# Five PSUM banks in turn behind the last sampling, and coarser steps beside the samplings

## The chip, the cores and the metric

One core of one Trainium2 chip. The metric is the device time of one launch in microseconds (us), the median of the runs shown; one further execution was recorded by the hardware profiler.

## The reference, cut to what matters

Four residual layers on x of shape (4, 256, 64, 64), each behind a group norm:

```
x = x + L0(gn(x))   # 1x1 conv; 3x3 depthwise -> offsets and masks; bilinear sampling at
                    # 4 groups x 9 points of every pixel; out-projection; squeeze-excite; MLP
x = x + L1(gn(x))   # qkv 1x1 conv; 5x5 depthwise of all 768 channels; linear attention; projection
x = x + L2(gn(x))   # 3x3 conv, 256 -> 256, binarised weights
x = x + L3(gn(x))   # attention of 4096 queries over 1024 pooled keys, softmax
```

All of it is float32. The sampling of L0 reads 4096 x 9 x 4 table rows of 256 values per image, at addresses that the offsets decide.

## The kernel before, in words

The channels lie on the 128 partitions in two halves (`KT = 2`), pixels on the free axis, in blocks of 512 (`NB = 8`). The four images are worked on as a pipeline. `sample(n, ...)` is the sampling of image n: 293 rounds of 14 pixels x 9 points. A round is four indirect DMAs that GpSimd issues (L520, tile `g`, 7 buffers), 16 small matmuls that weigh and sum them (L527, tile `acc`), and, once every two rounds (`UR = 2`), a ScalarE copy `at` (L532), two TensorE transposes into `dp` (L537) and ScalarE copies into `dT` (L552). Rounds are grouped in 19 blocks of up to 224 pixels. At the end of a block the output projection (L560, tile `po`), an addition on VectorE (L564) and a scaling with a running sum on ScalarE (L569) follow; in the kernel before these three lie in successive rounds, for each of the two halves of the channels.

The rest of the work is written as Python generators that `yield` a cost at points where other work may be put in. `beside(steps, number, *works)` runs one round of the sampling, then advances each work until its costs add up to its share of the rounds gone by: beside image n's sampling stand the MLP of image n-1 (`feed`, first fifth of the rounds), L1 of image n-1 (`linear`, the other four fifths) and L2 and L3 of image n-2 (`second`, the same four fifths). `LINEAR`, `SECOND` and `OFFSETS` are the sums of the costs. Beside image 0's sampling stands the preparation (convolution, depthwise, offsets) of images 1 to 3.

During the four samplings the order on TensorE, VectorE, ScalarE and GpSimd is the order written (`manual_schedule`); SyncE's DMAs are free. Behind the last sampling (image 3's) no such order is set: the framework's scheduler orders the instructions of each engine by their place in the program and by when it believes them ready. This last part holds MLP and L1 of image 3 with L2 and L3 of image 2 beside them, and then L2 and L3 of image 3 alone.

L1's 5x5 depthwise is 25 VectorE instructions of 128x1024 for each of 24 tiles of an image (L176, tile `agg`, in PSUM). At each of its steps L1 also takes one piece from a list `later`: transposes and sums (`vk`), or the output's parts `dens`, `head`, `proj` (L788 to L812). L2's convolution is 18 matmuls for each of 16 PSUM tiles (L864), whose result VectorE adds to the residual (L855). L3's attention is, for each of 32 groups of 128 queries: scores `s` (L943), VectorE maxima `mx` (L944, L945), ScalarE exponentials `pe` (L950), transposes `pt` (L958) with ScalarE copies `pT` (L959), and the sum over keys (L963).

PSUM has eight banks. The pool `mm` has three, shared by every common tile that `ps()` gives out; `acc` and `dp` of the sampling have one each, each used as two halves in turn; `agg` has two and `vk` one. Behind the last sampling `acc` and `dp` are idle.

Of the kernel before, what the change touches and what calls it, by code (L numbers as in the profile page):

```python
# [9 lines left out]
F32 = mybir.dt.float32  # L10
# [7 lines left out]
P = 128  # L18
# [17 lines left out]

CONVOLVE, OFFSETS = NB * 17 + 18, NCH * 60
FEED = NB * 40 + 8  # L40
LINEAR = 1130
SECOND = 631
EPS_BN = 1e-5
EPS_GN = 1e-5
EPS_ATT = 1e-5
# [24 lines left out]
class Net:  # L70
    def __init__(self, ctx, tc, a, out):
        self.tc, self.nc, self.a, self.out = tc, tc.nc, a, out
        e = ctx.enter_context
        self.cp = e(tc.tile_pool(name="const", bufs=1, side="left"))
        self.gp = e(tc.tile_pool(name="gather", bufs=2, side="left"))
        self.sp2 = e(tc.tile_pool(name="samp", bufs=2, side="left"))
        self.ps1 = e(tc.tile_pool(name="ps1", bufs=1, space=PSUM))
        self.mm = e(tc.tile_pool(name="mm", bufs=3, space=PSUM))
        self.dp = e(tc.tile_pool(name="scratch", bufs=1, space=DRAM))


    def ps(self, name="ps"):
        return self.mm.tile([P, 512], F32, name=name, tag="mm")

    def rsqrt(self, pool, v, eps, cols, name):

# [82 lines left out]
    def depthwise(self, acc, src, w, k, rows, cols, r0, bias=None, step=lambda cost: cost):  # L169

        nc = self.nc
        for t in range(k * k):
            s = src[:, r0 + t // k:r0 + t // k + rows, t % k:t % k + cols]
            wt = w[:, t:t + 1]
            if t:
                nc.vector.scalar_tensor_tensor(acc, s, wt, acc, ALU.mult, ALU.add)  # L176
            elif bias is not None:
                nc.vector.tensor_scalar(acc, s, wt, bias, ALU.mult, ALU.add)
            else:
                nc.vector.tensor_scalar(acc, s, wt, None, ALU.mult)  # L180
            if t % 3 == 2 or t == k * k - 1:
                yield step(3.9)


    def setup(self):
# [208 lines left out]
    def offsets(self, n, c, y, mw, bp, used):  # L394

        nc = self.nc
        t = bp.tile([P, KT, 1024], F32, name="t", bufs=1)
        for k in range(KT):
            acc = self.ps1.tile([P, 16, W], F32, name="agg", tag="agg")
            yield from self.depthwise(acc, y[:, k], self.w3[:, k], 3, 16, W, 0, bias=self.sh[:, 2 + k:3 + k])  # L400
            yield 2
            nc.scalar.activation(t[:, k], acc.rearrange("p r w -> p (r w)"), AF.Identity, scale=SLOPE)
            yield 2
            nc.vector.tensor_tensor(t[:, k], acc.rearrange("p r w -> p (r w)"), t[:, k], ALU.max)  # L404
            yield 3
        used.append(c)
        off = bp.tile([P, CT, 2 * Q], F32, name="off")
        ml = bp.tile([P, CT, Q], F32, name="ml")
        for h in range(2):
            ps = self.ps().rearrange("p (j o) -> p j o", o=P)  # L410
            for j in range(4):
                at = (4 * h + j) * P
                for k in range(KT):
                    nc.tensor.matmul(ps[:, j, 0:3 * Q], t[:, k, at:at + P], mw[:, k], start=k == 0, stop=k == KT - 1)  # L414
            ob = self.row("offmask_b").unsqueeze(1).to_broadcast([P, 4, 3 * Q])
            nc.vector.tensor_tensor(off[:, 4 * h:4 * h + 4], ps[:, :, 0:2 * Q], ob[:, :, 0:2 * Q], ALU.add)
            nc.vector.tensor_tensor(ml[:, 4 * h:4 * h + 4], ps[:, :, 2 * Q:3 * Q], ob[:, :, 2 * Q:3 * Q], ALU.add)
            yield 3
        yield from self.coordinates(bp, n, c, off, ml)
# [56 lines left out]
    def sample(self, n, ssum):  # L476
# [3 lines left out]

        nc, sp = self.nc, self.sp2
        table = self.tab[n].rearrange("g y x s c -> (g y x) (s c)")
        blocks, images, at, dp, dT, po, later = {}, {}, {}, {}, {}, {}, {}

        def halves(name):

# [52 lines left out]
        def spread(unit, b, u):  # L539

            if b not in dT:
                p0, np_ = BLOCKS[b]
                dT[b] = sp.tile([P, G, BP], F32, name="dT", bufs=1)
                images[b] = sp.tile([P, KT, BP], F32, name="yb")
                nc.sync.dma_start(images[b][:, :, 0:np_], self.y_d[n][:, :, p0:p0 + np_])
            full = sum(1 for _, m in unit if m == RP)
            for v0, v1, m in ((0, full, RP), (full, len(unit), unit[-1][1])):
                for s in range(2):
                    if v0 < v1:
                        hs = slice(64 * s, 64 * s + 64)  # L550
                        q0 = RP * (unit[0][0] + v0)
                        nc.scalar.copy(  # L552
                            dT[b][hs, :, q0:q0 + m * (v1 - v0)].rearrange("p g (v o) -> p g v o", o=m),
                            dp[u][hs, v0:v1, :, s, 0:m].rearrange("p v g o -> p g v o"))

        def project(b, m):
            np_ = BLOCKS[b][1]
            po[m] = self.ps("po")
            for k in range(G):
                nc.tensor.matmul(po[m][:, 0:np_], self.ow[:, k, m * P:(m + 1) * P], dT[b][:, k, 0:np_], start=k == 0, stop=k == G - 1)  # L560

        def add(b, m):
            ym = images[b][:, m, 0:BLOCKS[b][1]]
            nc.vector.tensor_tensor(ym, po[m][:, 0:BLOCKS[b][1]], ym, ALU.add)  # L564

        def finish(b, m):
            p0, np_ = BLOCKS[b]
            ym = images[b][:, m, 0:np_]
            nc.scalar.activation(ym, ym, AF.Identity, bias=self.sh[:, 4 + m:5 + m],  # L569
                                 scale=self.inv[:, 4 + m:5 + m], accum_out=ssum[:, m, b:b + 1])  # L570
            if m == KT - 1:
                nc.sync.dma_start(self.x2_d[n][:, :, p0:p0 + np_], images[b][:, :, 0:np_])

        load(0)
        order = [(b, r) for b, (_, np_) in enumerate(BLOCKS) for r in range(-(-np_ // RP))]
# [1 line left out]
        for i, (b, r) in enumerate(order):  # L577
# [14 lines left out]
            if r % UR == UR - 1 or ends:  # L592
                unit = rounds[r - r % UR:r + 1]
                todo = [partial(moved, acc, len(unit), i), partial(turned, len(unit), i), partial(spread, unit, b, i)]
                todo = list(enumerate(todo, i + 1))
                if ends:
                    todo += [(i + 4 + m + j, partial(f, b, m)) for m in range(KT) for j, f in enumerate((project, add, finish))]
                for j, f in todo:
# [235 lines left out]
    def layer2(self, n, st, st3):  # L834
        nc, tc = self.nc, self.tc
        with tc.tile_pool(name=f"ca{n}", bufs=1, side="left") as sp, \
# [4 lines left out]
            before = []  # L841
            for b in range(NB):

                lo, hi = max(8 * b - 1, 0), min(8 * b + 9, H)
# [9 lines left out]
                def leave(m, ps, xv, b):  # L854
                    nc.vector.tensor_tensor(xv[:, m], xv[:, m], ps, ALU.add)  # L855
                    if m == KT - 1:
                        self.stats(st3, xv, b)
                        nc.sync.dma_start(self.x5_d[n][:, :, b * 512:(b + 1) * 512], xv)

                for m in range(KT):  # L860
                    ps = self.ps()
                    for i in range(KT * 9):
                        k, t = i // 9, i % 9
                        nc.tensor.matmul(ps, w[:, k, t, m * P:(m + 1) * P], xp[:, k, t // 3:t // 3 + 8, t % 3:t % 3 + W],  # L864
                                         start=i == 0, stop=i == KT * 9 - 1)
                        if i % 3 == 2:
                            if before:
                                before.pop()()
                            yield 2.7
                    before.append(partial(leave, m, ps, xv, b))  # L870
            before.pop()()


    def layer3(self, n, st):
        nc, tc, a = self.nc, self.tc, self.a
        M = HW // 4
        with tc.tile_pool(name=f"na{n}", bufs=1, side="left") as sp, \
# [59 lines left out]
            for b in range(NB):  # L937
                m2 = bp.tile([P, 512], F32, name="m2")
                for j in range(4):
# [3 lines left out]
                        nc.tensor.matmul(s[i], tv[:, 4 * b + j], ph[:, i * 512:(i + 1) * 512], start=True, stop=True)  # L943
                        nc.vector.tensor_reduce(mx[:, i:i + 1], s[i], AX.X, ALU.max)  # L944
                    nc.vector.tensor_scalar(mx[:, 2:3], mx[:, 0:1], mx[:, 1:2], -1.0, ALU.max, ALU.mult)  # L945
                    yield 1.5
                    pe = bp.tile([P, M], F32, name="pe")
                    den = bp.tile([P, 3], F32, name="den3")
                    for i in range(2):
                        nc.scalar.activation(pe[:, i * 512:(i + 1) * 512], s[i], AF.Exp, bias=mx[:, 2:3], accum_out=den[:, i:i + 1])  # L950
# [23 lines left out]
    def run(self):  # L974
# [159 lines left out]
```

## Time and profile before

| | |
|---|---|
| median of 3 runs | 8708.86 us (8706.62 to 8726.91) |
| profiled execution: its own time | 8708.86 us |
| profiled execution: span, first to last instruction | 8706.8 us |
| gathers of image 0, 1, 2, 3: first to last | 247.6-1870.4, 1870.8-3399.2, 3399.5-5066.3, 5066.6-6749.1 us |
| busy over the span: TensorE, VectorE, ScalarE, GpSimd | 73%, 60%, 23%, 53% |
| mean granted TensorE clock | 0.836 |

The shares are means over stages that are bound by different things: GpSimd works only until 6749 us, so the kernel has two parts, the samplings and the 1958 us behind them, and each is to be read by itself.

### The profile page before, as it was taken

The page shows a single profiled execution, that of the slowest core. Times are in us where ns is not written, and L with a number is a line of the kernel's source. Part 1 is how long each engine was busy: PE and PEld are TensorE (multiplying, and loading weights), DVE is VectorE, ACT ScalarE, POOL GpSimd, SP SyncE. Part 2 cuts the span into 40 slices and gives each one's busy share as a digit, 9 for nine tenths or more (in the row PEclk, how much of TensorE's full clock was granted, in tenths as well). Part 3 has the DMA queues.
Part 4 walks back from the last instruction along what each step waited for, and adds up shares of the span by engine and source line. Part 5 has one row for each costly group of instructions (what it writes and reads, how often), then busy time and mean ns, then how long its engine had stood idle before and what let it go on. Part 6 is the DMA issues. An engine that isn't in the chain of part 4 may idle for free. (4 is left out here: it accounts for less than half of the span.)

```text
span 8706.8 us, 92673 instructions
## 1 busy us (share of the span) xinstructions
PE 6339.9 (73%) x35276; PEld 3432.2 (39%) x35276; DVE 5243.8 (60%) x6279; ACT 2014.2 (23%) x4710; POOL 4578.5 (53%) x4694
## 2 busy tenths in 40 slices
PE   4645545569676677998767779897677898667887
PEld 2333322334333333444444434444444444334345
DVE  7445353342678775258777732778777268989213
ACT  1111111112222122222232322222322222222113
POOL 0667767677777776777776557777755000000000
PEclk7666766779767688999988989998888999889999
DMA  5556555554444454455544354555433211101210
GB/s 157 165 153 170 152 154 157 142 156 144 136 120 127 119 145 136 144 155 140 155 132 119 111 150 137 159 150 152 126 111 107 90 53 46 44 32 41 57 60 29
DMA packets 817660, 1052.57 MB, mean 121 GB/s; under 512 B 464064, under 2 KB 524608, under 8 KB 815424
## 3 DMA queue, kind: packets, MB, share of 16 engines
q0 software_dynamic: 225024, 614.77, 24.4%
q1 hardware_dynamic: 592192, 431.89, 17.3%
q8 instruction: 279, 4.57, 0.2%
q14 instruction: 165, 1.35, 0.0%
HBM read 878.36 MB, written 167.90 MB: 120 GB/s over the span
## 5 line engine op out<-in xcount | busy, mean ns | idle before, releaser
L520 POOL DMA_INDIRECT g<-tab,sl x4688 | 4577.8, 976 | 2169.9 <-issue 1295.2
L176 DVE SCALAR_TENSOR_TENSOR agg<-pad,vec,agg 128x1024 f32<-128x1024 f32 x2560 | 3295.3, 1287 | 69.1
L527 PE MATMUL acc<-g,wm 128*32 128x128 f32 x18752 | 1221.6, 319 | 1186.6 <-ACT at L532 762.0
L527 PEld LDWEIGHTS acc<-g,wm 128*32 128x32 f32 x18752 | 609.5, 121 | 1845.7 <-ACT at L532 984.7
L864 PE MATMUL ps<-xp,w 128*128 128x512 f32 x2304 | 1062.3, 608 | 80.7 <-DVE xp L848 52.8
L864 PEld LDWEIGHTS ps<-xp,w 128*128 128x128 f32 x2304 | 425.7, 192 | 565.5 <-issue 530.8
L552 ACT COPY dT<-dp 64x112 f32<-64x112 f32 x1176 | 287.1, 244 | 1328.9 <-PE dp L537 935.3
L511 DVE TENSOR_TENSOR wm<-con,sl 128x1024 f32<-128x1024 f32 (+1 forms) x296 | 357.5, 1208 | 223.5 <-PE acc L527 221.3
L645 PE MATMUL ps<-x2f,f 128*128 128x512 f32 x1024 | 477.3, 615 | 4.0 <-ACT f L636 4.0
L167 DVE SCALAR_TENSOR_TENSOR hm<-ps,vec,lk 128x512 f32<-128x512 f32 x256 | 192.2, 751 | 436.2 <-ACT lk L166 436.1
L652 PE MATMUL ps<-hm,f 128*128 128x512 f32 x1024 | 453.6, 597 | 0.0
L166 ACT ACTIVATE lk<-ps,low 128x512 f32<-128x512 f32 x320 | 219.8, 687 | 980.9 <-PE ps L645 558.2
L700 PE MATMUL ps<-xr,qw 128*128 128x512 f32 x768 | 418.1, 675 | 12.3 <-DMA xq<-x 3.2
L958 PE MATMUL pt<-ident,pe 128*128 128x128 f32 x1024 | 187.6, 330 | 228.2 <-ACT pe L950 226.1
L950 ACT ACTIVATE pe<-s,mx 128x512 f32<-128x512 f32 x256 | 173.8, 684 | 712.9 <-DVE mx L945 712.8
L414 PE MATMUL ps<-mw,t 128*128 128x108 f32 x512 | 96.5, 364 | 306.9 <-DVE t L404 306.9
L963 PE MATMUL ps<-gt,pT 128*128 128x128 f32 x2048 | 309.6, 314 | 5.6 <-ACT pT L959 3.1
L963 PEld LDWEIGHTS ps<-gt,pT 128*128 128x128 f32 x2048 | 287.9, 224 | 49.4 <-ACT pT L959 20.0
L653 DVE TENSOR_TENSOR xyf<-xyf,ps 128x512 f32<-128x512 f32 x64 | 44.0, 688 | 430.9 <-PE ps L652 430.9
L560 PE MATMUL po<-dT,ow 128*128 128x224 f32 (+1 forms) x1216 | 284.6, 383 | 24.6 <-DVE yb L564 13.2
L532 ACT COPY at<-acc 128x256 f32<-128x256 f32 (+1 forms) x588 | 218.5, 372 | 313.9 <-PE acc L527 304.8
L645 PEld LDWEIGHTS ps<-x2f,f 128*128 128x128 f32 x1024 | 192.1, 194 | 233.2 <-issue 224.5
(224 smaller groups left out, 7096.4 us busy)
## 6 DMA issues: line engine op xcount, KB each, us to landing
x<-x SPq DMA_DIRECT2D x160, 512.0 KB
g<-tab,sl POOLq DMA_INDIRECT x4688
xr<-x SPq DMA_DIRECT2D x96, 512.0 KB
x<-in_x SPq DMA_DIRECT2D x64, 512.0 KB
tab<-xo SPq DMA_DIRECT2D x512, 64.0 KB
y<-yc SPq DMA_DIRECT2D x32, 512.0 KB
x2f<-x SPq DMA_DIRECT2D x32, 512.0 KB
xyf<-x SPq DMA_DIRECT2D x32, 512.0 KB
```

The costliest lines, as they stand in the source:

```text
L166: nc.scalar.activation(t, ps, AF.Identity, bias=low, scale=SLOPE)
L176: nc.vector.scalar_tensor_tensor(acc, s, wt, acc, ALU.mult, ALU.add)
L511: nc.vector.tensor_tensor(wm[:, 0:nu], self.con("own").unsqueeze(1).unsqueeze(1).to_broadcast(sh), sl[:, r:r + nu, G:].unsqueeze(3).to_bro ...
L520: nc.gpsimd.indirect_dma_start(out=g[:, i, :], out_offset=None, in_=table, in_offset=bass.IndirectOffsetOnAxis(ap=sl.bitcast(I32)[:, r, i: ...
L527: nc.tensor.matmul(acc[32 * i:32 * i + 32, :], wm[:, r4, 4 * i + 2 * x:4 * i + 2 * x + 2, :], g[:, i, x * P:(x + 1) * P], start=x == 0, st ...
L552: nc.scalar.copy(dT[b][hs, :, q0:q0 + m * (v1 - v0)].rearrange("p g (v o) -> p g v o", o=m), dp[u][hs, v0:v1, :, s, 0:m].rearrange("p v g ...
L560: nc.tensor.matmul(po[m][:, 0:np_], self.ow[:, k, m * P:(m + 1) * P], dT[b][:, k, 0:np_], start=k == 0, stop=k == G - 1)
L645: nc.tensor.matmul(ps, f1[:, k, m * P:(m + 1) * P], x2[:, k], start=k == 0, stop=k == KT - 1)
L652: nc.tensor.matmul(ps, f2[:, k, m * P:(m + 1) * P], hm[:, k], start=k == 0, stop=k == 4 * KT - 1)
L700: nc.tensor.matmul(ps, qw[:, k, t * P:(t + 1) * P], x[:, k], start=k == 0, stop=k == KT - 1)
L864: nc.tensor.matmul(ps, w[:, k, t, m * P:(m + 1) * P], xp[:, k, t // 3:t // 3 + 8, t % 3:t % 3 + W], start=i == 0, stop=i == KT * 9 - 1)
L963: nc.tensor.matmul(ps[:, 0:P], pT[:, m], gt[:, m], start=m == 0, stop=m == 7)
```

## The change: what it does

It is two edits in opposite places. First, behind the last sampling `ps()` hands out banks in the turn `mm, acc, mm, dp, mm`, five in all, where it was the three of `mm` throughout. Second, the fine steps of the kernel before are replaced by coarser ones:

- a depthwise yields after 5 taps where it yielded after 3 (in L1 and in the preparation), and two yields around the preparation's activation go;
- L2's convolution is two steps of 9 matmuls for each tile where it was six of 3, and the addition L855 follows its own tile's last matmul at once, where it lay behind the third matmul of the next tile;
- L3's exponentials follow the maxima in the same step, where a yield of 1.5 lay between;
- the block's projection, addition and scaling come in one round, for both halves of the channels one after the other, into the halves of the bank `dp` and no longer into `mm`; the residual tile `yb` has one buffer where it had two;
- the sums `OFFSETS`, `LINEAR` and `SECOND` are set to the new costs.

```diff
-CONVOLVE, OFFSETS = NB * 17 + 18, NCH * 60
+CONVOLVE, OFFSETS = NB * 17 + 18, NCH * 55
-LINEAR = 1130
-SECOND = 631
+LINEAR = 1068
+SECOND = 612
...
+        self.banks = cycle(["mm"])
     def ps(self, name="ps"):
-        return self.mm.tile([P, 512], F32, name=name, tag="mm")
+        tag = next(self.banks)
+        return (self.mm if tag == "mm" else self.ps1).tile([P, 512], F32, name=name, tag=tag)
...
-            if t % 3 == 2 or t == k * k - 1:
-                yield step(3.9)
+            if t % 5 == 4 or t == k * k - 1:
+                yield step(6.5)
...
-            yield 2
             nc.scalar.activation(t[:, k], acc..., AF.Identity, scale=SLOPE)
-            yield 2
...
-                images[b] = sp.tile([P, KT, BP], F32, name="yb")
+                images[b] = sp.tile([P, KT, BP], F32, name="yb", bufs=1)
...
-        def project(b, m):
-            np_ = BLOCKS[b][1]
-            po[m] = self.ps("po")
+        def project(b):
+            for m in range(KT):
+                projected(b, m)
+        def projected(b, m):
+            (p0, np_), yb = BLOCKS[b], images[b]
+            po = next(dps)
             for k in range(G):
-                nc.tensor.matmul(po[m][:, 0:np_], ...)
-        def add(b, m):
...
-        def finish(b, m):
+                nc.tensor.matmul(po[:, 0:np_], ...)
+            nc.vector.tensor_tensor(ym, po[:, 0:np_], ym, ALU.add)
             nc.scalar.activation(ym, ym, AF.Identity, ...)
...
-                if ends:
-                    todo += [(i + 4 + m + j, partial(f, b, m)) for m in range(KT) for j, f in enumerate((project, add, finish))]
+                for j, f in enumerate(todo + [partial(project, b)] * ends, i + 1):
...
-                        if i % 3 == 2:
-                            if before:
-                                before.pop()()
-                            yield 2.7
-                    before.append(partial(leave, m, ps, xv, b))
+                        if i == 8:
+                            yield 8
+                    nc.vector.tensor_tensor(xv[:, m], xv[:, m], ps, ALU.add)
+                    yield 8
...
-                    yield 1.5
...
-                    yield 2
+                    yield 3
...
+        self.banks = cycle(["mm", "acc", "mm", "dp", "mm"])
         beside(range(64), 64, *behind(N - 1), (second(N - 2), SECOND, 0.2, 1))
```

More of the change, by code (lines that the diff above doesn't have):

```diff
@@ L482, in sample @@
         table = self.tab[n].rearrange("g y x s c -> (g y x) (s c)")
-        blocks, images, at, dp, dT, po, later = {}, {}, {}, {}, {}, {}, {}
+        blocks, images, at, dp, dT, later = {}, {}, {}, {}, {}, {}
         def halves(name):
@@ L554, in spread @@
                             dp[u][hs, v0:v1, :, s, 0:m].rearrange("p v g o -> p g v o"))
-        def project(b, m):
-            np_ = BLOCKS[b][1]
-            po[m] = self.ps("po")
-            for k in range(G):
-                nc.tensor.matmul(po[m][:, 0:np_], self.ow[:, k, m * P:(m + 1) * P], dT[b][:, k, 0:np_], start=k == 0, stop=k == G - 1)
-        def add(b, m):
-            ym = images[b][:, m, 0:BLOCKS[b][1]]
-            nc.vector.tensor_tensor(ym, po[m][:, 0:BLOCKS[b][1]], ym, ALU.add)
-        def finish(b, m):
-            p0, np_ = BLOCKS[b]
-            ym = images[b][:, m, 0:np_]
+        def project(b):
[4 more added lines that the diff above has]
+            po = next(dps)
+            for k in range(G):
+                nc.tensor.matmul(po[:, 0:np_], self.ow[:, k, m * P:(m + 1) * P], dT[b][:, k, 0:np_], start=k == 0, stop=k == G - 1)
+            ym = yb[:, m, 0:np_]
+            nc.vector.tensor_tensor(ym, po[:, 0:np_], ym, ALU.add)
             nc.scalar.activation(ym, ym, AF.Identity, bias=self.sh[:, 4 + m:5 + m],
@@ L571, in finish @@
             if m == KT - 1:
-                nc.sync.dma_start(self.x2_d[n][:, :, p0:p0 + np_], images[b][:, :, 0:np_])
+                nc.sync.dma_start(self.x2_d[n][:, :, p0:p0 + np_], yb[:, :, 0:np_])
         load(0)
@@ L594, in sample @@
                 todo = [partial(moved, acc, len(unit), i), partial(turned, len(unit), i), partial(spread, unit, b, i)]
-                todo = list(enumerate(todo, i + 1))
-                if ends:
-                    todo += [(i + 4 + m + j, partial(f, b, m)) for m in range(KT) for j, f in enumerate((project, add, finish))]
-                for j, f in todo:
+                for j, f in enumerate(todo + [partial(project, b)] * ends, i + 1):
                     later.setdefault(j, []).append(f)
@@ L840, in layer2 @@
             sc, bi = yield from self.groupnorm(sp, st, "g2")
-            before = []
             for b in range(NB):
@@ L853, in layer2 @@
                 xv = self.block(bp, self.x4_d[n], b, "x4")
[L854 to L858, printed above, removed]
                 for m in range(KT):
@@ L865, in layer2 @@
                                          start=i == 0, stop=i == KT * 9 - 1)
-                        if i % 3 == 2:
-                            if before:
-                                before.pop()()
-                            yield 2.7
-                    before.append(partial(leave, m, ps, xv, b))
-            before.pop()()
+                        if i == 8:
+                            yield 8
+                    nc.vector.tensor_tensor(xv[:, m], xv[:, m], ps, ALU.add)
+                    yield 8
+                self.stats(st3, xv, b)
+                nc.sync.dma_start(self.x5_d[n][:, :, b * 512:(b + 1) * 512], xv)
     def layer3(self, n, st):
```

## The prediction, made before the changed kernel ran

> **What bounds the kernel now.** I first read the list of costliest groups, then split the span into stages and asked for the busy time of each engine in them, since the page's shares mix stages.
>
> ```profile
> 247.60:1870.40 1622.80, 881.71 (x6278) 518.38 (x6278) 718.76 (x962) 249.10 (x686) 1151.40 (x1172) 0.67 0.56 155
> 1870.40:3399.20 1528.80, 1103.95 (x6733) 544.32 (x6733) 996.56 (x969) 343.00 (x855) 1145.37 (x1173) 0.77 0.46 134
> 3399.20:5066.30 1667.10, 1341.03 (x8404) 726.65 (x8397) 1099.17 (x1274) 456.68 (x1102) 1141.77 (x1172) 0.91 0.47 137
> 5066.30:6749.00 1682.70, 1351.96 (x8479) 733.57 (x8478) 1104.47 (x1288) 463.52 (x1116) 1139.19 (x1172) 0.91 0.48 138
> 6749.00:7044.00 295.00, 268.62 (x768) 125.42 (x766) 88.64 (x152) 66.73 (x116) 0.05 (x1) 0.96 0.25 77
> 7044.00:7438.00 394.00, 344.09 (x1005) 171.60 (x1006) 338.05 (x346) 83.32 (x149) 0.00 (x0) 0.92 0.17 49
> 7438.00:8138.00 700.00, 475.49 (x1662) 280.36 (x1661) 582.99 (x710) 195.63 (x379) 0.00 (x0) 0.84 0.12 38
> ...
> 8404.00:8706.80 302.80, 220.41 (x1040) 154.69 (x1040) 98.22 (x256) 108.03 (x232) 0.00 (x0) 0.94 0.14 46
> ```
>
> The columns are stretch, length, then busy time (and count) of PE, PEld, DVE, ACT, POOL, then clock and DMA. Rows 1 to 4 are the samplings of images 0 to 3 (S0 to S3). POOL is busy some 1142 us in each and spends about 0.3 us of issue between two gathers (332.8 us in S1), so a sampling cannot be shorter than about 1470 us, 5.02 us a round. S1 is 55 us above this floor, S0 150, S2 and S3 about 200. Next I asked what POOL, PE and ACT waited for in S3 (us in total, times, longest):
>
> ```profile
> POOL g L520 <- PE acc L527: 212.8, 88, 10.9
> PE acc L527 <- ACT at L532: 167.6, 76, 14.7
> ACT pe L950 <- DVE mx L945: 187.3, 22, 18.1
> ```
>
> This is a chain. POOL waits for a free `g`, which PE frees; PE waits for ACT's copy of `acc`; ACT stands in front of an exponential whose maximum VectorE has not reached. By time, POOL's waits lie in the first rounds and, some 115 us of them, in the last 59 rounds, where L1's output and L3's attention meet. Two pairs of stretches from there, and L2's convolution beside S3:
>
> ```profile
> 6334.00:6429.00 95.00, 80.70 (x408) 40.07 (x409) 64.33 (x79) 30.56 (x70) 46.83 (x49) 0.90 0.37 108
> 6429.00:6465.00 36.00, 19.85 (x172) 14.91 (x170) 34.76 (x40) 8.61 (x24) 24.14 (x25) 0.86 0.38 114
> 6465.00:6559.00 94.00, 78.70 (x405) 39.45 (x406) 62.26 (x79) 28.54 (x65) 46.07 (x49) 0.91 0.36 104
> 6559.00:6593.00 34.00, 20.66 (x171) 14.55 (x170) 33.26 (x37) 10.29 (x28) 22.75 (x25) 0.80 0.44 132
> 5534.00:5948.00 414.00, 376.91 (x2355) 192.26 (x2358) 328.73 (x320) 108.01 (x266) 314.43 (x324) 0.97 0.52 147
> ```
>
> 49 gathers are 12 rounds: where the pieces of L1's output are taken, a round lasts 7.8 us and PE is 85% busy; where they have run out, it lasts 5.8 us and DVE is 97% busy. Beside the convolution POOL does not wait (324 gathers in 414 us is 5.1 us a round), although PE is 91% and DVE 79% busy: the seven buffers `g` hide short stalls.
>
> Behind the samplings the MLP is PE's (rows 5), the mixed stretch 7044 to 8138 is DVE's (921 of 1094 us), the convolution alone PE's, and the last attention nobody's: PE 73%, DVE 32%. Its timeline, one group of queries:
>
> ```profile
> 8562.53 1.98 PE L943 MATMUL s<-ph,th 128*128 128x512 f32 x4
> 8565.58 0.69 ACT L950 ACTIVATE pe<-s,mx 128x512 f32<-128x512 f32 x1 [4.38 <-DVE mx L945]
> 8566.42 1.33 PE L958 MATMUL pt<-ident,pe 128*128 128x128 f32 x8 [1.90 <-ACT pe L950]
> 8567.80 2.05 PE L963 MATMUL ps<-gt,pT 128*128 128x128 f32 x16
> ```
>
> Scores, exponential, transposes, sum, then the next group's scores: 7.17 us to the next `pt`, of which PE idles 1.9.
>
> **What the Trainium skill says.** "PSUM — Partial Sum Buffer", section on bank collisions: two engines may not use one bank in the same quadrant at a time, at other addresses of it either, so such accesses must be kept apart by waits. The trace agrees: PE, about to write one half of `acc`, waits for ACT's copy of the other (the 167.6 us above). The same page, section "Engine vs sequencer instructions": the queues of ScalarE, VectorE and GpSimd are strict first-in first-out; the 187.3 us of ACT and the copies behind them are that. "Perfetto Trace Analysis", "Optimizing Scalar/DVE Operations": where these engines aren't saturated but cause bubbles on others, breaking work up may let it complete sooner. Here that holds for DVE (65% over S3), and the change goes the other way. The same page, "Identifying Performance Opportunities": a repeating gap can mean too little PSUM for the next tile. The 1.9 us above repeats 32 times; no run shows yet that banks are its cause.
>
> **The change part by part**, against the profiled execution's own 8708.9 us (span 8706.8; the median is the same execution). No engine's arithmetic changes; all costs are waits.
>
> *Exponentials with their maxima.* The second work is given 631/(0.8 x 293) = 2.69 units a round, so the yield of 1.5 put the exponential behind a round's boundary in 1.5/2.69 = 56% of the cases: 18 of 32 groups of an image lose that. ACT then waits while VectorE does the chunk written before, 5 x 1.29 = 6.5 us, and the maxima, 2 x 0.68 + 0.21 = 1.6 us. Half of them stand before a copy `at`, which PE needs. In the last 59 rounds (10 of the 18) I take 5 us each for 5 of them, elsewhere `g` hides most: 30 us an image in S2 and S3. Bounds: 0 (VectorE ahead) and 18 x 8.1 = 146.
>
> *Projection at once and in `dp`.* Its 8 matmul records a half, the addition (0.38 us) and the scaling are the same. New is that PE's second half, and the next transposes `dp`, wait for VectorE's additions in the same bank: at least about 0.6 us twice a block, plus VectorE's lag, 0 to 6.5 us, say 3, where it is busy. Behind PE stand the matmuls of `acc`; behind ACT, whose scaling waits likewise, the copies `at`. About 4.2 us of PE for each of 14 blocks beside L1 in S2 and S3; the last four count in full (17), the rest is in PE's idle time and `g`: 20 an image, 8 in S1, 7 in S0. SP's load of `yb` now waits for the store of the block before, but is wanted 11 rounds later: nothing, unless other loads queue behind it; that would add a few us. Bounds: 0 and 19 x 8 = 152 a sampling.
>
> *Five taps a step.* VectorE is up to 2 x 1.29 = 2.6 us later with everything behind a chunk: weights `wm`, maxima, additions. About ten places in the last rounds: 25 us an image. Against it, `later` gives one piece a step, and steps come less often: 4.56/6.5 = 0.70 a round, before 4.83/3.9 = 1.24. The 13 pieces of an output take 15.5 rounds of 18, before 10. PE's need, (80.70 + 19.85)/18.5 = 5.4 us a round, would be even, as would DVE's, (64.33 + 34.76)/18.5 = 5.4. If nothing stalled, the last rounds would fall from 7.0 to 5.4: 59 x 1.6 = 95 us an image gained. In-order waits keep most of it; I take a third, -30. In the preparation the steps already come in one burst, since it waits for its tiles and catches up; nothing there.
>
> *Convolution in two steps.* 288 matmuls take 279 us an image, so a step is 8.7 us of PE, before 2.9. VectorE's addition now stands in its queue until its own tile is done: up to 8 us, 16 times, with chunks of the depthwise queued behind. The stretch has 414 - 329 = 85 us of VectorE idle per image, which covers most: 20 an image; bounds 0 and 80. Two of the three `mm` banks are less held, worth a few us.
>
> *Banks behind the samplings.* In the last attention, five tiles a group and five banks let the next scores start once the exponentials have read theirs. If both go ahead of the sum, the group is PE-bound, 1.98 + 1.33 + 2.05 = 5.4 us: 32 x 1.8 = 57 us gained. If the scheduler puts only the first ahead, 5 to 10; if none, 0. I take 30. In the mixed stretch DVE idles 173 us, about 46 of them in the drain after the last depthwise tile and some 40 in two holes; I take 20, bounds -20 and 60 (the fixed turn can also make a tile wait for one held bank, and the coarser steps move the order). MLP and convolution alone: nothing, PE is full.
>
> Sum: S2 and S3 each 30 + 20 + 25 - 30 + 20 = 65, S0 and S1 15 together: +145; behind them -50. 8708.9 + 95 = 8804 us.
>
> **The rivals.** *Evenness wins* (faster): the spread of L1's pieces pays for all new waits. Then the samplings are level (S2, S3 at -10 each, S0 and S1 +10) and the part behind gives 57 + 20: 8709 - 10 - 77 = 8622 us. For it: the 7.8 and 5.8 us rounds side by side. Against: every piece still passes a chain PE, ACT, DVE in order, and DVE at 5.4 us a round has no slack. It decides when the samplings lose less than the attention gains. *The banks change no order* (the change doesn't do what it says): the exponential is still waited for by the transposes, the gain behind is 0: 8709 + 145 = 8854 us. *Lockstep* (much slower): waits for projection, exponentials and convolution sums add up as PE and DVE both run above 90%; S2 and S3 lose 130 each: 8709 + 275 - 40 = 8944 us. *A draw*: loss and gain cancel.
>
> **How the numbers follow.** A measurement of this kernel can tell about 0.3%, 26 us, from no change. Chances: 0.48 for the forecast (own range 8740 to 8870), 0.15 for no new order, 0.08 for lockstep, 0.20 for evenness, 0.09 for a draw. Slower 0.71, same 0.09, faster 0.20. The range reaches into the faster case and most of the way to lockstep: 8640 to 8920.
>
> **What would show it.** POOL's wait for PE `acc` should rise from 192.6 (S2) and 212.8 (S3) to about 260 to 280 each, ACT's wait for `mx` above 187.3, DVE's wait for PE at L855 above 23.4, and PE or ACT should wait for DVE at the projection's addition. The 7.8 and 5.8 us rounds should move together. Behind the samplings, PE's wait for `pe` at L958 in the last attention, now
>
> ```profile
> PE pt L958 <- ACT pe L950: 63.0, 32, 4.0
> ```
>
> should fall, with `s` of the next group before L963. I am wrong if the samplings don't lengthen, or if that wait stays and the last stretch keeps its 303 us.

## The result, and the profile after

The changed kernel takes 9070.43 us (median of 4 runs, 9065.32 to 9074.08) against 8707.74 us for the kernel before (4 runs): ratio 1.0412, 95% interval 1.0394 to 1.0430. It is slower, by 363 us, where 95 were forecast. The profiled execution, one of the four, has a span of 9067.9 us, 361 more than before's 8706.8 (also one of its four).

In the views PE is TensorE, DVE is VectorE, ACT is ScalarE and POOL is GpSimd. The four samplings again, S0 to S3, with the columns of the prediction's first table:

```profile
247.70:1877.10 1629.40, 878.66 (x6260) 513.84 (x6260) 722.29 (x967) 252.13 (x689) 1152.29 (x1172) 0.68 0.55 155
1877.40:3407.40 1530.00, 1056.57 (x6734) 529.30 (x6734) 997.85 (x964) 342.46 (x852) 1151.31 (x1172) 0.77 0.46 133
3407.70:5242.30 1834.60, 1366.87 (x8401) 743.53 (x8399) 1104.81 (x1273) 455.03 (x1098) 1139.72 (x1172) 0.87 0.43 124
5245.50:7105.90 1860.40, 1386.67 (x8460) 756.29 (x8459) 1110.05 (x1287) 461.46 (x1112) 1139.98 (x1172) 0.87 0.43 125
```

S0 is 7 us longer, S1 1 us, S2 168 and S3 178. The part behind the last gather is 1962 us where it was 1958. So nearly the whole loss lies in the two samplings that have L1, L2 and L3 beside them, and the five banks gave nothing that shows in the sum. Over the span the busy time of VectorE, ScalarE and GpSimd is the same as before to 1%; what grew is waiting. The chain of S3's waits, the same three as before:

```profile
POOL g L521 <- PE acc L528: 397.4, 101, 17.1
PE acc L528 <- ACT at L533: 212.0, 101, 14.0
ACT pe L938 <- DVE mx L934: 251.3, 31, 17.2
```

POOL's wait rose from 212.8 to 397.4 us, by 185, which covers the 178 us. PE's for the copy `at` rose by only 44. To see where, I cut S3 by rounds, at the same rounds in both kernels: 66 to 166 (L2's convolution runs), 166 to 234, 234 to 293. First the kernel before, then the changed one:

```profile
5454.00:5975.00 521.00, 461.15 (x2849) 237.00 (x2848) 401.33 (x420) 139.22 (x339) 389.78 (x400) 0.95 0.53 151
5975.00:6334.00 359.00, 233.41 (x1904) 160.05 (x1903) 291.42 (x341) 112.25 (x281) 263.98 (x272) 0.84 0.47 136
6334.00:6749.00 415.00, 320.86 (x1863) 170.74 (x1864) 303.54 (x357) 118.53 (x281) 228.61 (x236) 0.89 0.37 108
```

```profile
5641.00:6272.00 631.00, 483.36 (x2834) 252.62 (x2834) 388.49 (x394) 137.94 (x337) 388.95 (x401) 0.87 0.43 122
6272.00:6675.00 403.00, 240.86 (x1921) 165.90 (x1921) 309.08 (x369) 114.23 (x286) 266.16 (x272) 0.81 0.43 126
6675.00:7106.00 431.00, 323.09 (x1846) 171.66 (x1846) 304.19 (x356) 116.11 (x274) 225.75 (x236) 0.86 0.36 104
```

The last 59 rounds, in which the forecast put most of its loss, are 16 us longer. The 68 rounds before them are 44 longer, and the convolution's 100 rounds 110. By the same cuts, with the first 66 rounds in front, POOL's wait for PE is 57.1, 13.9, 16.9 and 124.9 us before and 66.5, 128.4, 57.9 and 144.6 us after: in every stretch its growth (9, 114, 41 and 20 us) is the growth in length (8, 110, 44 and 16 us) to a few us.

In the convolution's rounds PE is busy 22 us more (some matmul records are longer; the granted clock is 0.87 where it was 0.95) and idle 148 us where it was 60. Before the change these 100 rounds stood at 5.2 us, close to GpSimd's pace of 5.02, and PE had only those 60 us in which to make up for a wait. What it waits for there, changed kernel first, then before:

```profile
PE ps L853 <- DVE xp L843: 55.5, 5, 13.5
PE acc L528 <- ACT at L533: 32.2, 30, 2.6
PE dp L565 <- DVE yb L567: 24.4, 6, 11.8
PE pt L738 <- ACT av L719: 19.8, 3, 9.5
```

```profile
PE ps L864 <- DVE xp L848: 26.3, 5, 12.0
PE acc L527 <- ACT at L532: 10.6, 7, 4.5
```

Three of the four end at VectorE: `xp` are the border zeros of the next convolution tile, `yb` the projection's addition, `av` a copy of a finished depthwise. VectorE is busy for only 388 of the 631 us there; it stands still itself, for PE. At the convolution's addition, after and before:

```profile
DVE x L857 <- PE ps L853: 117.4, 13, 29.0
DVE x L855 <- PE ps L864: 23.4, 5, 6.8
```

At the projection's addition it stands 56 us, before 25.7. One such wait in its timeline:

```profile
5772.96 0.24 DVE L380 MEMSET pad<- 128x40 f32 x4
5797.90 0.39 DVE L567 TENSOR_TENSOR yb<-dp,yb 128x224 f32<-128x224 f32 x1 [24.70 <-ACT kt L740]
5800.17 0.39 DVE L567 TENSOR_TENSOR yb<-dp,yb 128x224 f32<-128x224 f32 x1 [1.87 <-PE dp L565]
```

VectorE had run ahead of TensorE, met the addition of a projection that TensorE had not reached, and stood 24.7 us with the whole depthwise queued behind it. The wait is for several semaphores, and the view names another one; the projection's first half, which the addition reads, ends at 5797.8, 0.1 us before the addition starts. A second fragment shows the exponentials' part of the chain, at 6462 us, one view for each engine:

```profile
6462.21 11.89 DVE L179 SCALAR_TENSOR_TENSOR agg<-pad,vec,agg 128x1024 f32<-128x1024 f32 x9
6475.57 0.69 ACT L938 ACTIVATE pe<-s,mx 128x512 f32<-128x512 f32 x1 [12.38 <-DVE mx L934]
6477.43 0.37 ACT L533 COPY at<-acc 128x256 f32<-128x256 f32 x1
6477.85 1.08 PE L528 MATMUL acc<-g,wm 128*32 128x128 f32 x16 [13.02 <-ACT at L533]
```

Nine depthwise instructions, then the maxima, then the exponential for which ScalarE has waited 12.4 us, then the copy behind it, then TensorE, idle for 13 us.

Behind the samplings, from before to after, cut by line: MLP 222.4 to 221.6 us, the mixed stretch (end of the MLP to the last convolution) 1114.4 to 1119.0, the convolution alone 250.5 to 249.5, the last attention 266.4 to 258.6. In the attention only half of the next group's scores moves ahead of the sum: in the changed kernel's timeline `s` takes two records before L951 and two after it, and a group takes 6.77 us, before 7.17. TensorE's wait for the exponentials is what it was (63.0 us before):

```profile
PE pt L946 <- ACT pe L938: 63.3, 32, 3.2
```

### The profile page after: what moved, and what is told of

Its sections match the earlier page's. It is cut to its first block, busy times and chain, and to the rows that moved or that the text cites. A ratio compares the mean times of both kernels' runs of the same rounds, so it can differ in the third digit from the quotient of the medians.

```text
span 9067.9 us, 92807 instructions
## 1 busy us (share of the span) xinstructions
PE 6356.0 (70%) x35276; PEld 3456.7 (38%) x35276; DVE 5259.2 (58%) x6279; ACT 2013.6 (22%) x4710; POOL 4584.1 (51%) x4694
## 5 line engine op out<-in xcount | busy, mean ns | idle before, releaser
L528 PE MATMUL acc<-g,wm 128*32 128x128 f32 x18752 | 1151.8, 318 | 1161.5 <-ACT at L533 794.2
L528 PEld LDWEIGHTS acc<-g,wm 128*32 128x32 f32 x18752 | 588.4, 121 | 1742.3 <-ACT at L533 1020.5
L565 PE MATMUL dp<-dT,ow 128*128 128x224 f32 (+1 forms) x1216 | 324.8, 421 | 153.5 <-DVE yb L567 152.1
L565 PEld LDWEIGHTS dp<-dT,ow 128*128 128x128 f32 x1216 | 264.0, 231 | 212.2 <-DVE yb L567 180.7
L932 PE MATMUL s<-ph,th 128*128 128x512 f32 x512 | 285.1, 663 | 56.1 <-DVE x L959 40.9
L857 DVE TENSOR_TENSOR x<-x,ps 128x512 f32<-128x512 f32 x64 | 43.9, 686 | 469.7 <-PE ps L853 469.7
L951 PE MATMUL ps<-gt,pT 128*128 128x128 f32 x2048 | 304.8, 311 | 1.5 <-ACT pT L947 0.8
L951 PEld LDWEIGHTS ps<-gt,pT 128*128 128x128 f32 x2048 | 287.4, 222 | 48.2 <-issue 31.1
```

Source lines behind the costliest of these rows:

```text
L528: nc.tensor.matmul(acc[32 * i:32 * i + 32, :], wm[:, r4, 4 * i + 2 * x:4 * i + 2 * x + 2, :], g[:, i, x * P:(x + 1) * P], start=x == 0, st ...
L565: nc.tensor.matmul(po[:, 0:np_], self.ow[:, k, m * P:(m + 1) * P], dT[b][:, k, 0:np_], start=k == 0, stop=k == G - 1)
L951: nc.tensor.matmul(ps[:, 0:P], pT[:, m], gt[:, m], start=m == 0, stop=m == 7)
```

## The experiments

The chips differ in pace. On one (before 8721 us) a round of the sampling takes about 5.2 us as in the profiles shown; on others (before 9806 to 9846 us) the same program takes about 6 us a round in the samplings. Ratios are always to the kernel before on the same chip, with the 95% interval in brackets; differences in us are of medians. Stretches in rounds are compared at one pace only. The runs at the slower pace have no profile of the kernel before; where a zero of a stretch is needed there, it is taken from runs whose edits don't touch it, and is good to some 10 us: 620 to 630 us for rounds 66 to 166, 421 for 166 to 234 and 429 for 234 to 293.

**e1: the convolution alone**, on a slower chip.

```diff
-                        if i % 3 == 2:
-                            if before:
-                                before.pop()()
-                            yield 2.7
-                    before.append(partial(leave, m, ps, xv, b))
...
+                        if i == 8:
+                            yield 8.1
+                    nc.vector.tensor_tensor(xv[:, m], xv[:, m], ps, ALU.add)
+                    yield 8.1
```

> The kernel before with L2's convolution alone as in the changed kernel: two steps of 9 matmuls for each tile, the addition L855 straight behind its own tile's last matmul (the two yields are 8.1 each, so that SECOND stays 631). Theory (lost head start): an addition queued in the round of its own matmuls makes VectorE wait for TensorE, the depthwise behind it stands still, and TensorE then waits for VectorE at xp and at the transposes; most of the 108 us that rounds 66 to 166 of S2 and of S3 got longer lies here: 130 to 220 us over both samplings, with VectorE's wait for TensorE at the addition near 100 us an image, and S0, S1 and the part behind as before. Rival (the prediction's own price): VectorE's idle time covers the wait and the loss is about 20 us an image, 40 in all. Second rival (projection at once is the cause): under 30 us.

9959.26 us, before 9833.40: 1.0120 (1.0078 to 1.0161), +126 us, a little under the theory's 130 to 220. Rounds 66 to 166 take 684 and 681 us in S2 and S3, against 621 in e4, which leaves the convolution alone. The prediction's price of 40 us falls.

**e2: the projection at once alone**, same chip.

```diff
-                images[b] = sp.tile([P, KT, BP], F32, name="yb")
+                images[b] = sp.tile([P, KT, BP], F32, name="yb", bufs=1)
...
-            po[m] = self.ps("po")
...
+            po = next(dps)
...
-                    todo += [(i + 4 + m + j, partial(f, b, m)) for m in range(KT) for j, f in enumerate((project, add, finish))]
...
+                for j, f in enumerate(todo + [partial(project, b)] * ends, i + 1):
```

> The kernel before with the block's projection alone as in the changed kernel: projection, addition and scaling of both halves in one round, in the halves of the bank dp, yb with one buffer. Theory (lost head start): VectorE waits in its queue for the projection of the same round, up to 25 us where it had run ahead; 60 to 130 us over S2 and S3 together, in rounds 66 to 234, with VectorE's wait at L564's counterpart above 50 us an image, S0 and S1 under 10 us each. Rival (the prediction's price): TensorE waits for VectorE's lag, 20 us an image, 40 to 55 in all. Second rival (only the convolution matters): under 20 us.

9917.39 us: 1.0087 (1.0064 to 1.0110), +84 us. The size is the theory's, the place only in part: S0 takes 2085 us where e1 has 2050, so some 35 us of it fall beside the preparation. In S2 and S3 rounds 66 to 166 take 638 and 639 us and 166 to 234 take 427 and 431, some 20 us an image over the zeros, which is the prediction's price for these two samplings.

**e3: exponentials with their maxima alone**, same chip.

```diff
-SECOND = 631
+SECOND = 615
...
-                    yield 1.5
                     pe = bp.tile(...)
...
-                    yield 2
+                    yield 3
```

> The kernel before without the yield between L3's maxima and exponentials (SECOND 615). The prediction's price is 30 us an image, 60 us in all, in the last 107 rounds of S2 and S3, with ScalarE's wait for mx up from 187 us. Theory (lost head start in convolution and projection is nearly all of the loss): under 30 us, since the last 59 rounds of the changed kernel were only 16 us longer. It may also be slightly faster than before.

9933.44 us: 1.0102 (1.0075 to 1.0130), +100 us (74 to 128 by the interval). My theory that the convolution and the projection are nearly all of the loss falls, and the prediction's 60 is too low for the whole. Where the exponentials run it is nearly right: rounds 234 to 293 take 453 and 449 us, e1 429 and 429, and rounds 166 to 234 take 433 in the mean, e1 421, so some 34 us an image. Where the rest lies isn't known without a profile of the kernel before at this pace.

**e4: the depthwise in steps of 5 alone**, same chip.

```diff
-CONVOLVE, OFFSETS = NB * 17 + 18, NCH * 60
+CONVOLVE, OFFSETS = NB * 17 + 18, NCH * 55
...
-LINEAR = 1130
+LINEAR = 1068
...
-            if t % 3 == 2 or t == k * k - 1:
-                yield step(3.9)
+            if t % 5 == 4 or t == k * k - 1:
+                yield step(6.5)
...
-            yield 2
...
-            yield 2
```

> The kernel before with the depthwise alone in steps of 5 taps, without the two yields in the preparation (LINEAR 1068, OFFSETS 55 a chunk). The prediction's price: 25 us lost by a later VectorE and 30 gained by evener pieces of L1's output, so about -10 us over S2 and S3. Theory: between -40 and +40 us, with the last 59 rounds of S2 and S3 shorter and rounds 66 to 234 longer. Rival (chunk length is the cause of the loss): over 100 us, in rounds 66 to 166.

9868.68 us: 1.0036 (1.0027 to 1.0045), +35 us. This is inside the theory's range, near its upper end. But the last 59 rounds are 437 and 434 us, not shorter than e1's 429: no gain from spreading the pieces of L1's output shows.

**e5: the kernel before once more**, no edit, now on a chip of the profile's pace.

> The kernel before, unchanged, for its stages on this run's chip: on the chip of the first four experiments a round of the sampling took about 6.2 us where it took 5.2 in the profile shown, so stages are to be compared on one chip. No theory is at stake; equal to the runs of before beside it.

8728.80 us (one run) beside 8721.43. Rounds 66 to 166 of S2 and S3: 523 and 520 us; 166 to 234: 366 and 363.

**e6: early addition, fine steps**, same chip.

```diff
-                        if i % 3 == 2:
-                            if before:
-                                before.pop()()
+                        if i % 3 == 2 and i < KT * 9 - 1:
                             yield 2.7
-                    before.append(partial(leave, m, ps, xv, b))
+                    leave(m, ps, xv, b)
+                    yield 2.7
```

> The kernel before with six steps of 3 matmuls kept, but the addition L855 straight behind its own tile's last matmul. Theory (the place of the addition costs, since VectorE stands still for TensorE): most of what the coarse convolution cost in the first set (126 us) is back, 70 to 140 us, with VectorE's wait at L855 as there. Rival (the length of the step costs, since 9 matmuls hold up the sampling's matmuls for 8.7 us): under 40 us.

8777.69 us: 1.0069 (1.0049 to 1.0089), +56 us, between the theory's 70 to 140 and the rival's 40; 14 us an image in rounds 66 to 166, 5 to 12 in 166 to 234. VectorE's wait at this addition in S3 is 56.9 us, in e5 23.4, and TensorE's for `xp` 47.4 against 26.3.

**e7: long steps, late addition**, same chip.

```diff
-                        if i % 3 == 2:
+                        if i % 9 == 8:
                             if before:
                                 before.pop()()
-                            yield 2.7
+                            yield 8.1
```

> The kernel before with two steps of 9 matmuls for each tile, but the addition left until behind the next tile's first 9. Theory (place of the addition): under 50 us of loss. Rival (length of the step): 70 to 140 us.

8812.42 us: 1.0109 (1.0088 to 1.0129), +91 us; 44 us an image in rounds 66 to 166 and none elsewhere. The rival is right here: the length of TensorE's step costs more than the place of the addition. The addition also comes six matmuls later than in the kernel before, but this isn't what costs: in these rounds of S3 VectorE waits 3.0 us at it, and no instruction waits for it. e7's own waits of TensorE in that stretch of S3:

```profile
PE ps L864 <- DVE xp L848: 48.0, 6, 13.8
PE acc L527 <- ACT at L532: 32.8, 30, 3.8
```

The second is the changed kernel's line almost to the number (32.2, 30 times), and in e6, with short steps, it is 10.6 us in 7 waits, as before the change, so that wait comes with the long step. (My reading, not tested: after nine matmuls in a row the copies and the next round's matmuls meet in short succession.) VectorE stands still for TensorE here too, at other places: 63.3 us at the sampling's weights `wm` and 48.5 at the projection's addition, where e5 has 30.2 and 25.8. POOL's wait for PE in the 100 rounds is 14.6 us in e5, 29.3 in e6 and 57.3 in e7.

**e8: the five banks alone**, same chip.

```diff
+        self.banks = cycle(["mm"])
...
-        return self.mm.tile([P, 512], F32, name=name, tag="mm")
...
+        tag = next(self.banks)
+        return (self.mm if tag == "mm" else self.ps1).tile([P, 512], F32, name=name, tag=tag)
...
+        self.banks = cycle(["mm", "acc", "mm", "dp", "mm"])
         beside(range(64), 64, *behind(N - 1), (second(N - 2), SECOND, 0.2, 1))
```

> The kernel before with the five banks behind the last sampling alone. The samplings are the same instructions in the same order. From the changed kernel's own trace: the last attention 8 us shorter (266.4 to 258.6), the mixed stretch between -20 and +10 us, so -25 to +5 us in all, not to be told from no change. The prediction's -50 would need the next group's scores ahead of the sum over keys.

8714.93 us: 0.9995 (0.9986 to 1.0005), no change (-12 to +4 us by the interval). Its profile has 255.8 us in the last attention, 11 less than the profile of before, and 1113.9 in the mixed stretch.

**e9 to e12: the changed kernel with one edit undone**, on a slower chip (before 9805.65 us). The edits are those of e1 to e4, taken back.

> The changed kernel with L2's convolution as before (six steps of 3, addition behind the next tile's third matmul; SECOND 615). Theory (one shared reserve: in rounds 66 to 166 TensorE has about 40 us of idle time below GpSimd's pace, each edit spends it, and all waits beyond it count in full): undoing the convolution takes back more than its price alone, 120 to 200 us of the 361, so 8870 to 8950 us where before is 8708, with rounds 66 to 166 back under 560 us. Rival (prices add up; 44 + 14 us an image seen alone): 115 us.

> The changed kernel with projection, addition and scaling in three rounds and in mm as before, yb with two buffers. Theory (shared reserve): 100 to 180 us back, in rounds 66 to 234, with VectorE's waits for the projection (97 us in S3) back near 31. Rival (prices add up; 0.87% alone on the slow chip): 75 to 85 us.

> The changed kernel with the yields of 1.5 and 2 around L3's exponentials (SECOND 628). Alone on the slow chip this edit cost 1.0%, where the prediction said 60 us. Theory: 20 to 90 us back, in rounds 186 to 293 only; nothing in rounds 66 to 166, where no exponential runs. Rival (its cost is covered by the other waits of these rounds): under 20 us.

> The changed kernel with the depthwise in steps of 3 taps and the preparation's two yields (LINEAR 1130, OFFSETS 60 a chunk). Theory (shared reserve): 30 to 120 us back, mostly in rounds 66 to 234, since a chunk of 6.5 us on VectorE stands before each addition and each xp that TensorE waits for. Rival (evener pieces of L1's output are worth more than the longer chunk costs): the last 59 rounds of S2 and S3 get longer, and under 20 us come back in all.

Left of the loss: without the convolution's edit 1.0200 (1.0155 to 1.0245), without the projection's 1.0192 (1.0163 to 1.0222), without the exponentials' 1.0242 (1.0213 to 1.0272), without the depthwise's 1.0266 (1.0236 to 1.0296). The 8870 to 8950 us that e9 was to show belong to the other pace and can't be compared. Nor was the changed kernel run at this pace, so what each undoing gives back wasn't measured. An estimate from two later runs (209 us for all edits but the convolution's in e16, 96 to 126 for that one in e13 and e1) puts the whole loss here at 305 to 335 us; the four remainders are 184 to 256, so each edit is probably worth undoing. The convolution's stretch falls to 625 and 632 us only in e9, and stays at 683 to 690 in the other three; the last 59 rounds are shortest without the exponentials' edit (438 and 435 us). Without the depthwise's they take 451 and 458 us, and with it 453 and 452 (e9, whose own edit lies in other rounds), so evener pieces don't show a gain here either.

**e13 to e16: sums**, on a slower chip (before 9846.30 us). e13 is e1's kernel, e14 e2's, e15 has both edits, e16 is e9's kernel.

> The kernel before with L2's convolution coarse and its addition early, as in the first experiment, now beside the next three on one chip. On a chip of the profile's pace both theories say more than the parts seen alone (44 + 14 us an image in rounds 66 to 166): shared reserve 60 to 90 us an image, adding prices 58.

> The kernel before with the projection at once, as in the second experiment. In rounds 66 to 166: shared reserve under 15 us an image, since alone it stays within TensorE's idle time; adding prices: 25 to 50. In rounds 166 to 234: 10 to 40 us if it is the one that lengthens them.

> The kernel before with both the convolution coarse and the projection at once. Adding prices: the losses of the two runs before this one, summed, stretch by stretch. Shared reserve: in rounds 66 to 166 at least 20 us an image more than that sum, near the 108 of the changed kernel.

> The changed kernel with the convolution as before. Shared reserve: rounds 66 to 166 within 15 us of before (the other edits alone stay in the reserve) and rounds 166 to 234 still 30 to 60 us longer, since no convolution runs there. Adding prices: rounds 66 to 166 some 50 us longer than before.

1.0114 (1.0050 to 1.0177), 1.0076 (1.0053 to 1.0099), 1.0232 (1.0173 to 1.0291) and 1.0229 (1.0170 to 1.0287). In time, +96, +70, +212 and +209 us. The two alone make 166 and together 212, and the intervals hold both answers. In rounds 66 to 166 the prices add: 678 us (e13), 633 (e14) and 690 (e15), means of S2 and S3, with a zero of 620 to 630. A reserve that the two share, with 20 us more than the sum, isn't seen there at this pace. In rounds 166 to 234 it is otherwise: e16 takes 461 and 468 us, e13 (no edit that works there) 421. The projection alone makes 432, the exponentials 433 (e3), the depthwise 428 (e4): together some 43 us, singly about 10, 12 and 7, which is 29. Here the three edits cost more together than apart.

**e17 and e18: both kernels once more**, at the profile's pace again, so the slower chips' zero and whole were not measured.

> The kernel before once more, for its stretches beside the next run. On a slow chip rounds 66 to 166, 166 to 234 and 234 to 293 of S2 and S3 should take about 620, 422 and 430 us, if the runs that leave a stretch's edits out show it rightly.

> The changed kernel once more. On a slow chip: the four edits cost 96 to 126 (convolution), 70 to 84 (projection), 100 (exponentials) and 35 us (depthwise) alone there, 300 to 345 together, and 184 to 256 us are left when one is undone. Adding prices: about 300 to 330 us slower than before, and what each undoing gives back is what the edit cost alone. Shared reserve: the whole is above the sum, 350 us or more. On a chip of the profile's pace: 361 us within 30.

8729.10 us (one run) and 9064.44 us, the latter 1.0403 (1.0373 to 1.0433) of before's 8715.25, within the 361 us give or take 30 that were expected at this pace. The loss repeats, and by stretch to 4 us: rounds 66 to 166 take 627.6 and 627.2 us, 166 to 234 403.7 both times.

## Why the prediction was wrong in size

*The direction* was right: slower, no engine's work changed, the loss in S2 and S3, and POOL's wait for PE carries it. S0 and S1 together cost 8 us where 15 were said. The size was not: 346 us in S2 and S3 for 130, and 9070 lies above the range, which ended at 8920. The *lockstep* rival, with 8 in 100, came nearest and was still 126 us low.

*The place* was wrong. The terms put some 37 us an image into the last 59 rounds (25 of the exponentials, 17 of the projection, 25 less 30 of the five taps) and 20 beside the convolution; the trace has 16 and 110. *The path* was right in part: of the 148 us that PE idles beside the convolution, only 32.2 are the chain's link, the wait for ScalarE's copy. Most of the rest is for VectorE itself, at `xp` and the projection's addition.

*Which steps failed.* Two: the convolution's longer step, priced at nothing, and the plain sum of the terms. An image was to lose 20 by the projection, 30 by the exponentials, -5 by the taps and 20 by the convolution, 65 in all. Alone they lose in S2 and S3 some 20, 34, 13 and 58 to 66 (by stretches, an estimate from e1 to e7, the first three at the slower pace), about 130. Together they lose 173.

*Convolution in two steps* is the term that failed by most: 20 us an image. I wrote that a step is 8.7 us of PE and gave that no price at all; alone it costs 44 us an image in its stretch (e7). For the addition I took VectorE's 85 idle us as cover. Alone it costs 14 us in the stretch and 5 to 12 behind it (e6), near the 20. But VectorE's idle time was the wrong cover: while VectorE stands at an addition, what it owes PE stands behind it (in e6 PE's wait for `xp` is 47.4 us, in e5 26.3), and PE, with 60 idle us in these 520 where VectorE had 120, was the engine short of time.

*Projection at once*: 20 an image and 15 in S0 and S1, 55 in all. Alone, 70 to 84 us on the slower chips, but some 35 of them in S0, which in the changed kernel at the profile's pace is only 7 us longer; in S2 and S3 the price held. What I priced, PE's waiting for VectorE in the shared bank, is there: 40.8 us at the projection and 8.7 at the next transposes in S3, where 14 blocks of 4.2 us had been 59. What I left out is the other direction, VectorE's waiting for PE at this addition: 97 us in S3, before 31. Alone this costs little. That in the full set it delays `xp` and `av`, for which PE waits, is read from the trace; at the slower pace undoing the projection (e10) does not shorten the convolution's stretch.

*Exponentials*: 30 an image, 60 in all; alone +100 us on a slower chip, of which some 34 an image where exponentials run. The mechanism is the one described, and the fragment at 6462 us shows it. ScalarE's wait for `mx` in S3 rose from 187.3 us in 22 waits to 251.3 in 31: nine more waits of the same 8 us, where up to 18 were allowed for. The longest did not grow (18.1 and 17.2 us).

*Five taps a step*: the forecast was -5 an image; alone +35 us in all (e4), some 13 of them an image in the last 127 rounds of S2 and S3. The relief of 30 us by evener pieces isn't seen in e4 nor in the full set (e12 beside e9), and the rounds did not become even: in groups of three, the last 59 of S3 take 5.0 to 9.1 us before and 5.0 to 10.6 after.

*Banks*: -50 forecast, none measured (e8), and +4 us behind the samplings in the changed kernel. The term took about half of a 57 us gain. What happens is the case named as the small one (5 to 10 us): the first score goes ahead of the sum, the second does not, and the next exponential waits as long as before. In the mixed stretch nothing came. The Trainium skill's hint that a repeating gap can mean too little PSUM ("Perfetto Trace Analysis", section "Identifying Performance Opportunities") did not hold for this gap: with five banks PE's wait for the exponentials is 63.3 us (62.5 in e8), with three 63.0. Whether another order, with both scores ahead, would use the banks was not run.

*Two readings* were a little off and change nothing: POOL's waits in the last 59 rounds of S3 are 124.9 us, not 115, and the 7.17 us of a group hold where no output projection lies between two groups (the group shown is followed by one, and takes 9.48).

*Open*: at the profile's pace the convolution's stretch is 110 us longer, 58 of it seen in e6 and e7 apart. The other 50 were not taken apart there: they may be the projection, the depthwise, the convolution's own two halves together, or the interplay of all with a PE that has little time left. At the slower pace, where the stretch has more slack, all edits but the convolution's leave it at 625 to 638 us (e9, e16), within some 15 of its zero, and no interplay shows. That interplay is the larger part of the 50 is my guess, not shown.

## What to carry to other kernels

Where engines run written orders side by side, find the engine that is short of time in each stretch and price every edit by the waits it gives that engine; idle time of another engine is no cover. Prices found one at a time may not add: three edits that cost 10, 12 and 7 us alone cost 43 together in rounds 166 to 234 (e16). A consumer queued directly behind its producer costs the consumer's lead: leave it until the producer is surely done, as the kernel before did with the convolution's addition (e6, 56 us). And the length of a step between two time-critical rounds is a cost of its own: three matmuls or nine, with the same work, are 91 us apart (e7).

## What the runs showed of the hardware that was not expected

The same program takes 8702 to 8736 us on some chips and 9792 to 9864 on others, with the difference in the samplings: rounds 66 to 234 of S1, where e13 is still the kernel before, take 864 us in the profile of before and 999 in e13, while the part behind the last gather takes 1958 and 1972. Why is not known.

And TensorE's mean granted clock was lower where it waited more: 0.95 before, 0.92 in e7 and 0.87 after, over the same 100 rounds with the same matmuls (60, 95 and 148 us idle). Its busy time there is 461, 469 and 483 us. The median of the convolution's matmul records is the same in all three (592 ns), so it is a part of the records that got longer; that the clock is what made them longer was not tested.
